# Holding the second megabyte of block 0's tokens until the second 512 KB of its first megabyte has landed, instead of the first

## The chip, the cores and the metric

The kernel runs on one core of a Trainium2 chip. The metric is the device time of one execution in microseconds (us), as the median of several runs. All data is 32-bit floating point except the two lists of ids.

## The reference, cut to what matters

x holds 64 sequences of 64 tokens with 1024 features each. Every sequence has an adapter id and a language id.

```python
# layer 0: a rank-16 adapter chosen per sequence
Bx  = einsum('bni,bri->bnr', x, B0[ids0])
x   = x + einsum('bnr,bor->bno', Bx, A0[ids0])
# layer 1: a dense product, and eight rank-16 experts with a top-2 gate
base   = einsum('btd,od->bto', x, W)
logits = einsum('btd,ed->bte', x, Wr) + 5.0 * one_hot(ids1)
gates  = softmax over the two largest logits, 0 elsewhere
h      = einsum('btd,erd->bter', x, A1)
x      = x + base + 2.0 * einsum('bter,bte,eor->bto', h, gates, B1)
```

## The kernel before, in words

The 4096 tokens lie feature-major in memory (xT, 1024 x 4096) and are worked on in 8 blocks of 512 tokens. A block's tokens are 2 MB and arrive as two tiles x of 1 MB, for the lower and the upper half of the features. `load` (line 363) brings them in with DMAs that SP issues. The first tile of block 0 alone is cut into two DMAs of 512 KB. Two blocks form a super-block; the dense product W is computed on super-blocks with a scheme that makes seven products out of eight, some of them cut again in the same way.

For each block k the steps are these, by their names in the code and in the profile:

- `gather` (397): an indirect DMA that POOL issues fetches the block's adapter rows, gb (from the B table) and ga (from the A table), 512 KB each.
- `turn` (424): TensorE transposes gb in eight pieces into PSUM (pt), in two groups of four; ScalarE copies each group into bt.
- `project` (445): pb = bt times x, in two halves over the features, so the second half needs the second tile of x. VectorE masks pb into bx.
- `adapt` (477): px = ga times bx, once for the lower and once for the upper half of the features; VectorE adds px into x in four parts per half.
- `rows` (515): ph = x times a_sb (the experts' first matrices, and behind them wr_c, the router's weights), one strip of 128 tokens after the other. Then come the gates, and the products with W (pw, pa, pb, pf).

Two DMAs are held back by small copies on POOL. `hold` in `load` writes one column of the second tile of block 0's tokens with a value read from the first tile; the DMA that fills the second tile must come after this copy, and the copy after the data it reads. `hold` in `consts` (309) does the same for a_sb with a value of gb of block 0. `spread`, also in `consts`, copies wr_c behind a_sb on POOL.

The order of the instructions on each engine isn't the order of the code. Each step is given to a planner, the class `Plan`, with a cost for each engine that could do it, what it reads and writes, the buffers that it takes, and a due time `at` (lower is more urgent). `order` (64) goes through the steps with its own estimate of time, and each engine then executes its steps in that order. The estimates rest on constants: LAG 0.2 between engines, 350 KB per us for DMA with LAND 1.8 behind it, GATHER 1.5 for an indirect DMA before LAND, and start times SET for SP, DVE and POOL. Of the steps that an engine could start within LOOK (0.2) of the earliest one, it takes the one with the lowest due time (lines 140 and 141):

```python
t0 = min(can[e])[0][0]
_, n, t = min((steps[n]["at"], n, t) for (t, _), n in can[e] if t <= t0 + self.LOOK)
```

`behind` says that a step isn't planned before another one has begun. Block 0's ga is behind the second tile of x, block 1's gb behind a_sb, and so are block 1's tokens and W. The due times at the start: gb of block 0 -61, its x and ga -60, the hold of a_sb -56, a_sb and the spread -45, gb of block 1 -43, pt of block 0 -40, pb -38, px -37 and -36, ph -14 to -11, pt of block 1 -12. Of PSUM buffers there are four l (pt, pb, ph, and px of four parts at a time), two a and two b (px of block 0's upper half takes these four). There is one bt.

Of the kernel before, what the change touches and what calls it, by code (L numbers as in the profile page):

```python
# [174 lines left out]
def kernel(  # L175
# [58 lines left out]
    HC = NC // 2  # L234
# [19 lines left out]
    act, pool, sp = Pinned(tc, nc.scalar), Pinned(tc, nc.gpsimd), Pinned(tc, nc.sync)  # L254
# [14 lines left out]
    def new(tag, shape, name):  # L269
        return pools[tag].tile(shape, F32, tag=tag, name=name)  # L270
# [81 lines left out]
    made = {}  # L352

    def part(t, cs=range(HC), gs=range(NG)):
        return [(t, c, g) for c in cs for g in gs]
# [7 lines left out]
    def load(k, i, at):  # L363
        t = ("x", k, i)

        held = (k, i) == (0, 1)

        def hold(e):

            made[t] = new("q", [P, HC, TB], f"x_{k}_{i}")  # L370
            pool.tensor_copy(made[t][:, 0, :1], made["x", 0, 0][:, 0, :1])


        cuts = ((0, HC // 2), (HC // 2, HC)) if (k, i) == (0, 0) else ((0, HC),)

        def fn(c0, c1):
            if not held and c0 == 0:
                made[t] = new("q", [P, HC, TB], f"x_{k}_{i}")
            sp.dma_start(
                made[t][:, c0:c1],  # L380
                xT[(i * HC + c0) * P : (i * HC + c1) * P, k * TB : (k + 1) * TB].rearrange(
                    "(c p) t -> p c t", p=P
                ),
            )

        if held:
            plan.add(
                {"POOL": 0.2}, hold, part(("x", 0, 0), [0]), part(t), at, [("q", t)]
            )
        for c0, c1 in cuts:  # L390
            plan.add(
                {"SP": 0.5}, lambda e, c0=c0, c1=c1: fn(c0, c1),
                [], part(t, range(c0, c1)), at, [("q", t)] * (not held and c0 == 0),
                kb=256 * (c1 - c0), behind=[("a1",)] * (k == 1) + [(t, 0, 0)] * (c0 > 0),
            )
# [359 lines left out]
    def fine_weights(s, n, k, a, at):  # L755
# [33 lines left out]
        if s == FINE:  # L789
            for x in range(4):  # L790
                plan.add(
                    {"DVE": 0.29, "POOL": 0.48}, sums(x), [(a,)] + [(t, y) for y in range(x)], [(t, x)], at - 3,
                    [("s", t)] * (x == 0), sb=True,
                )
            plan.add({"SP": 0.1}, keep, [(t, x) for x in range(4)], [("fine", n, k)], at + 4, kb=256)
        else:
            plan.add({"SP": 0.1}, load, [("fine", n, k)], [(t, x) for x in range(4)], at - 6, [("s", t)], kb=256)
# [462 lines left out]
    for k, at in ((0, -60), (1, -42)):  # L1260
        load(k, 0, at)
        gather(k, "gb", b0, at - 1)
        load(k, 1, at)
        gather(k, "ga", a0, at)
        if k == 0:
            consts()
# [81 lines left out]
```

## Time and profile before

| | |
|---|---|
| median of 3 runs | 515.6 us (515.21 to 516.27) |
| profiled execution, its own time | 514.86 us |
| its span, first to last instruction | 513.0 us |
| TensorE (PE) busy | 499.8 us, 97% |
| VectorE (DVE) busy | 410.3 us, 80% |
| DMA | 110.00 MB, 214 GB/s on the mean |
| granted TensorE clock, mean | 0.999 |
| first matmul | 8.80 us after the span's start |

The times in the profile's views count from the start of the span of this one execution. It was 0.74 us quicker than the median of the runs. In a view of instructions in order of time, a line has the start, the duration, the engine, the operation and its tiles, and in brackets how long the engine sat idle before it and what released it. SPq is SP's queue of DMA issues; its durations are those of issuing, not of the transfer.

### The profile page before, as it was taken

The page shows a single profiled execution, that of the slowest core. Times are in us where ns is not written, and L with a number is a line of the kernel's source. Part 1 is how long each engine was busy: PE and PEld are TensorE (multiplying, and loading weights), DVE is VectorE, ACT ScalarE, POOL GpSimd, SP SyncE. Part 2 cuts the span into 40 slices and gives each one's busy share as a digit, 9 for nine tenths or more (in the row PEclk, how much of TensorE's full clock was granted, in tenths as well). Part 3 has the DMA queues.
Part 4 walks back from the last instruction along what each step waited for, and adds up shares of the span by engine and source line. Part 5 has one row for each costly group of instructions (what it writes and reads, how often), then busy time and mean ns, then how long its engine had stood idle before and what let it go on. Part 6 is the DMA issues. An engine that isn't in the chain of part 4 may idle for free.

```text
span 513.0 us, 9559 instructions
## 1 busy us (share of the span) xinstructions
PE 499.8 (97%) x3678; PEld 442.5 (86%) x3678; DVE 410.3 (80%) x822; ACT 75.8 (15%) x204; POOL 105.4 (21%) x175
## 2 busy tenths in 40 slices
PE   3999999999999999999999999999999999999997
PEld 2857888889888998889888998889989999999996
DVE  0788899989878777888989789874889988875964
ACT  1111100001000211111201221102301112112210
POOL 3002000020432433442233021201212120212100
PEclk9999999999999999999999999999999999999999
DMA  8999273964895648875567645972756665673023
GB/s 286 374 369 351 83 270 120 332 247 141 300 312 201 208 130 284 309 247 187 185 226 236 221 131 173 356 260 81 240 173 205 231 202 142 228 192 96 0 115 132
DMA packets 60172, 110.00 MB, mean 214 GB/s; under 512 B 5600, under 2 KB 11744, under 8 KB 60128
## 3 DMA queue, kind: packets, MB, share of 16 engines
q1 hardware_dynamic: 57824, 101.01, 58.7%
q0 software_dynamic: 2304, 8.39, 4.9%
q8 instruction: 29, 0.48, 0.4%
q14 instruction: 15, 0.12, 0.1%
HBM read 76.09 MB, written 33.29 MB: 213 GB/s over the span
## 4 chain that ended last, share of the span: by engine, by line
PE 94%; DMA 4%; DVE 1%; issue 0%; SPq 0%
PE pa L29 38%; PE pb L29 19%; PE pf L29 16%; PE ph L29 12%; PE px L29 3%; PE pw L29 3%; DMA x<-in_xT 3%; PE pt L29 2%; DMA gb<-in_b,idx 1%; PE pg L29 1%; DVE s L29 0%; DMA ids_sb<-in_ids 0%; DVE ti L29 0%; DVE u L29 0%; DVE x L29 0%
## 5 line engine op out<-in xcount | busy, mean ns | idle before, releaser
L29 PE MATMUL pa<-ti,s 128*128 128x256 f32 x432 | 102.1, 380 | 0.0
L29 PEld LDWEIGHTS pa<-ti,s 128*128 128x128 f32 x432 | 78.7, 190 | 9.3
L29 ACT COPY cp<-pf 128x128 f32<-128x128 f32 (+1 forms) x123 | 37.0, 302 | 214.4 <-PE pf L29 201.3
L29 PEld LDWEIGHTS ph<-a_sb,x 128*128 128x128 f32 x512 | 61.7, 190 | 1.5 <-issue 0.9
L29 PE MATMUL ph<-a_sb,x 128*128 128x136 f32 x512 | 62.5, 279 | 0.2 <-issue 0.2
L29 PE MATMUL pb<-ti,s 128*128 128x256 f32 x224 | 55.8, 380 | 0.0
L29 PE MATMUL pa<-x,s 128*128 128x256 f32 x216 | 52.7, 381 | 0.0
L29 PE MATMUL pf<-tt,sf 128*128 128x128 f32 x246 | 47.5, 277 | 0.0
L29 DVE TENSOR_TENSOR x<-px,x 128x512 f32<-128x512 f32 x64 | 39.9, 683 | 6.8 <-PE px L29 6.8
L29 PEld LDWEIGHTS pb<-ti,s 128*128 128x128 f32 x224 | 40.9, 190 | 4.8 <-issue 0.2
L29 PEld LDWEIGHTS pf<-tt,sf 128*128 128x128 f32 x246 | 41.4, 191 | 3.8 <-issue 0.4
L29 PEld LDWEIGHTS pa<-x,s 128*128 128x128 f32 x216 | 39.3, 190 | 5.0 <-issue 0.4
L29 PE MATMUL pa<-t,s 128*128 128x256 f32 x168 | 41.2, 380 | 0.0
L29 PEld LDWEIGHTS pa<-t,s 128*128 128x128 f32 x168 | 30.8, 190 | 3.9 <-issue 0.2
L29 POOL TENSOR_TENSOR tt<-ti 128x256 f32<-128x256 f32 x16 | 12.3, 771 | 93.5 <-PE pf L29 60.2
L29 DVE TENSOR_TENSOR o<-pa,u 128x512 f32<-128x512 f32 x32 | 22.0, 687 | 9.9 <-PE pa L29 9.6
L29 POOL TENSOR_TENSOR tt<-x 128x256 f32<-128x256 f32 x11 | 9.2, 833 | 93.9 <-PE pf L29 47.7
L29 DVE TENSOR_TENSOR o<-pb,o 128x512 f32<-128x512 f32 x35 | 23.1, 687 | 2.7 <-PE pb L29 1.9
L29 DVE TENSOR_TENSOR ti<-t 128x512 f32<-128x512 f32 x24 | 16.7, 696 | 8.4 <-PE pb L29 6.4
L29 DVE TENSOR_TENSOR ti<-x,ti 128x512 f32<-128x512 f32 x30 | 21.7, 724 | 1.2 <-PE pb L29 0.6
L29 DVE TENSOR_TENSOR o<-o,cp 128x256 f32<-128x256 f32 x46 | 19.6, 425 | 2.5
L29 POOL TENSOR_TENSOR sf<-s 128x128 f32<-128x128 f32 x27 | 14.0, 518 | 35.8 <-DMA s<-s_kept 14.5
(154 smaller groups left out, 807.6 us busy)
## 6 DMA issues: line engine op xcount, KB each, us to landing
s<-s_kept SPq DMA_DIRECT2D x147, 256.0 KB
x<-in_xT SPq DMA_DIRECT2D x15, 1024.0 KB
out_T<-o SPq DMA_DIRECT2D x30, 512.0 KB
s_kept<-s SPq DMA_DIRECT2D x28, 256.0 KB
sf<-f_kept SPq DMA_DIRECT2D x27, 256.0 KB
s_kept<-w SPq DMA_DIRECT2D x18, 256.0 KB
w<-in_w SPq DMA_DIRECT2D x16, 256.0 KB
f_kept<-sf SPq DMA_DIRECT2D x14, 256.0 KB
```

The lines of the kernel that those rows point to most:

```text
L29: return self._tc.keep_in_program_order(f(*args, **kwargs))
```

## The change

The hold of the second tile reads its value from another place of the first tile: from the first of the chunks that the second 512 KB bring (chunk HC // 2 = 2 of four), where it was chunk 0, of the first 512 KB. What the planner is told that the hold reads is changed with it. Nothing else is touched.

```diff
         def hold(e):

             made[t] = new("q", [P, HC, TB], f"x_{k}_{i}")
-            pool.tensor_copy(made[t][:, 0, :1], made["x", 0, 0][:, 0, :1])
+            pool.tensor_copy(made[t][:, 0, :1], made["x", 0, 0][:, HC // 2, :1])
...
         if held:
             plan.add(
-                {"POOL": 0.2}, hold, part(("x", 0, 0), [0]), part(t), at, [("q", t)]
+                {"POOL": 0.2}, hold, part(("x", 0, 0), [HC // 2]), part(t), at, [("q", t)]
             )
```

## The prediction

> **What bounds the kernel now.** I read the page first, then TensorE's busy time by stretches, then the chain of waits of the first 18 us, and last the order of PE, POOL and SP in those 18 us.
>
> The page's busy row, then the stretches (columns: stretch, length, busy time, instructions, granted clock, DMA share, GB/s):
>
> ```profile
> PE 499.8 (97%) x3678; PEld 442.5 (86%) x3678; DVE 410.3 (80%) x822; ACT 75.8 (15%) x204; POOL 105.4 (21%) x175
> ...
> 8.80:17.90 9.10, 8.52 (x144) 1.00 1.05 371
> 17.90:60.00 42.10, 42.06 (x333) 1.00 0.82 291
> 60.00:110.00 50.00, 49.70 (x314) 1.00 0.71 256
> 110.00:510.10 400.10, 399.56 (x2891) 1.00 0.61 198
> ```
>
> TensorE is the bound from 17.9 us on: over the 492.2 us to 510.1 it is idle 0.88 us. A moment at which its work is put off early in the kernel is hardly won back later. So the change is priced at one place: when does the first ph matmul start, now at 17.93 us? The chain says what stands before it:
>
> ```profile
> 3.08 5.59 DMA gb<-in_b,idx
> 8.66 0.14 issue
> 8.80 1.94 PE pt L29 x8
> 10.74 3.39 PE pb L29 x64
> ...
> 14.15 0.30 DVE bx L29
> ...
> 14.50 2.07 PE px L29 x64
> 16.56 1.18 PE pt L29 x8
> 17.74 0.19 issue
> 17.93 0.35 PE ph L29
> ```
>
> The first gather (gb of block 0) lands at 8.66 and starts TensorE. The px products of block 0 follow at 14.50, then pt, the eight transposes of block 1's gathered rows. Those fill a gap: ph waits for VectorE's additions of px into x, so 1.25 us of pt costs nothing where it stands. Now POOL and SP:
>
> ```profile
> 3.08 1.11 POOL L29 DMA_INDIRECT gb<-in_b,idx  x1 [1.31 <-DVE order L29]
> 5.06 0.18 POOL L29 COPY x<-x 128x1 f32<-128x1 f32 x1 [0.87 <-DMA x<-in_xT]
> 5.27 0.38 SPq L29 DMA_DIRECT2D x<-in_xT  x1
> 5.40 0.97 POOL L29 DMA_INDIRECT ga<-in_a,idx  x1 [0.16 <-issue]
> 6.59 0.24 POOL L29 COPY a_sb<-wr_c 128x64 f32<-128x64 f32 x1 [0.22 <-issue]
> 8.71 0.18 POOL L29 COPY a_sb<-gb 128x1 f32<-128x1 f32 x1 [1.88 <-DMA gb<-in_b,idx]
> 8.93 0.66 SPq L29 DMA_DIRECT2D a_sb<-in_a  x1
> 9.04 0.97 POOL L29 DMA_INDIRECT gb<-in_b,idx  x1
> ```
>
> The copy at 5.06 is the hold that is changed. Block 1's gather (9.04) has its own row, from issue to landing 6.6 us, so it lands at 15.64, just 0.85 us before TensorE takes up pt at 16.49:
>
> ```profile
> DMA to landing us min/median/max: 6.6/6.6/6.6
> ```
>
> **The change, part by part.** No instruction is added or taken away. The hold waits for the second 512 KB of block 0's first megabyte.
>
> *On the chip.* DMA moves 395 GB/s in the microsecond from 4.0, at which 512 KB take 1.33 us, and the two halves share one queue, the second behind the first. I put the hold at 6.3 instead of 5.06 (both ends: 6.0 and 6.5). Behind it on POOL stand the gather ga of block 0, the spread, the hold of a_sb, and block 1's gather; on SP the second megabyte, then a_sb, the first w and block 1's tokens. The second megabyte is issued at about 6.5, 1.2 us late.
>
> *In the order.* The planner works with its own guesses and fixes each engine's order by them; I use these only for the order, not for a time. Before: the first cut is thought to land at 4.96, hold at 5.16, second megabyte issued 5.56 and landed 10.93, hold of a_sb 7.50, block 1's gather issued 8.00 and landed 12.40. The second half of pb is put at 11.13 to 12.07, bx at 12.27 to 12.57, px at 12.77. pt of block 1 could start at 12.60 (landing plus LAG), 0.17 ahead of px: inside LOOK (0.2), so the lower due time wins and px goes first.
>
> After: the second cut is thought to land at 4.63 + 1.80 = 6.43; hold 6.63 to 6.83. The spread is ready and POOL takes it at 6.83 to 7.13, the second megabyte is issued at 7.03 and, at (7.53 + 2.93) + 1.80, landed at 12.25. ga takes POOL from 7.13 to 8.23, ahead of the hold of a_sb (its due time is lower), which comes at 8.23; a_sb is issued at 8.63, block 1's gather at 8.73, thought to land at 13.13. Second half of pb: 12.45 to 13.39. bx: 13.59 to 13.89. px: 14.09. But pt of block 1 is ready at 13.33, and can start at 13.59 (its bt buffer comes free with the end of pb, plus LAG). Now it is 0.50 ahead of px, outside LOOK, so pt goes first. It takes one of the four l slots; px of the first half needs all four, so the second pt follows too (14.03), then px of the second half, which uses the a and b slots, then px of the first half. TensorE's order becomes pb, pt, pt, px, px, ph. **This swap, not the 1.2 us, is what I price.**
>
> *The sum.* pt now stands in front of px and waits for block 1's gather. When does that land? From its issue: the first gather's landing barely moves, and POOL is at its hold by then, so issue is about 8.7 to 9.0, and 6.6 us later is 15.3 to 15.6. From the stream: DMA runs at about 370 GB/s from 7 to 18 us, the second megabyte leaves up to 1.2 us late, ga ahead of it on the same queue 1.4 us late: 15.64 + 1.2 = 16.8. I take the middle, 16.0. Then 0.14 to start (as at 8.66 to 8.80), 1.25 for eight transposes, and 14.50 to 17.93 = 3.43 from px to ph (two of VectorE's additions of one half and one of the other, as now): 16.0 + 0.14 + 1.25 + 3.43 = 20.82. Against 17.93 that is **+2.9 us**; +2.2 with 15.3, +3.7 with 16.8. With the shortest gather row (5.6 us) it would still be +1.2.
>
> What lies beside it costs nothing: the wait of pb's second half for the second megabyte (perhaps 0 to 0.7 us around 12.2) ends before the wait for the gather does, and an earlier start of TensorE is eaten by it as well. a_sb is needed only by ph and gets 2.9 us more; block 1's tokens and w likewise. If that cover were gone, a_sb's 512 KB at 1.4 us would be the price. From ph on TensorE's work is the same, so the sum stands to the end. The profiled execution took 514.86 us; with +2.9 it is 517.8. It lies 0.74 under the median of 515.6, so against runs like those I say **518.5**.
>
> *A rule against the trace.* Both groups are 64 matmuls of one shape, block 0's before 17.8 and block 1's after it (mean ns of one last, then idle before):
>
> ```profile
> L29 PE MATMUL pb<-x,bt 128*32 128x128 f32 x64 | 3.4, 402 | 0.0
> ...
> L29 PE MATMUL pb<-x,bt 128*32 128x128 f32 x64 | 2.0, 274 | 0.0
> ```
>
> The granted clock reads 1.00 in both places, yet the first runs at 53 ns each and the second at 31, and pt of block 0 took 1.94 where that of block 1 took 1.25. The Trainium skill, "TensorE: Matmul & The Clock Gate", section "Part 1: The HAM clock gate", says that the array starts at half rate and falls back to it after an idle window of some 3.4 us. TensorE would now idle from about 14.1 to 16.1. By the rule as stated 2.0 us are too short, so the fast durations above hold (+2.9). If it did fall back, pt costs 0.7 more and px 64 times 21 ns, 1.3: +4.9. I take the fast one.
>
> **The rivals.**
>
> *Not slower: the gather gains and the order stays.* Between 7.0 and 8.7 the second megabyte shares the engines with the tail of the first gather:
>
> ```profile
> q1 hardware_dynamic: 113, 0.23, 64.0%
> q0 software_dynamic: 51, 0.15, 36.6%
> ```
>
> This is the microsecond from 7.0; q0 is the gather. The skill's "DMA: Bandwidth & Descriptors", "Queues, rings and completion order", says that each engine goes round-robin between its queues. Alone, the 0.15 MB need 0.4 us at the 373 GB/s of that microsecond; the gather could land some 0.9 us sooner than 8.66 by the rule. The trace is less kind: its tail is short of bytes (0.01 MB after 8.0) and seems to hang on a slow ring, so I would give it 0.3. Then TensorE starts at 8.5 and pb's first half ends near 12.1. It decides whether px stays ahead of pt and whether the second megabyte has landed by 12.1: then -0.3, 515.3. Against it: the planned gap of 0.50 is well over LOOK.
>
> *Same order, and the second megabyte is the bound.* Now pb's two halves run without a gap. Issued 1.2 us later, the megabyte may land at 12.3 to 13.0, and pb waits 0.2 to 0.9 us: 516.1.
>
> *The swap, and TensorE falls back to the slow pace:* +4 to +5, 520.2. For it: the idle windows need not begin where the wait does, and the wait may be 2.7 us.
>
> *The edit does nothing*, if the hold waited for both halves already. It did not: by 5.0 us DMA had moved 0.20, 0.30 and 0.40 MB in the three microseconds from 2.0, and both halves are 1.05 MB.
>
> **How the numbers follow.** Swap at the fast pace 0.64, swap at the slow pace 0.18; order kept with the megabyte as bound 0.10; order kept with a gain 0.06; something else, such as the later order falling better, 0.02. The range, 516.4 to 520.6, holds the swap from +1.2 to +5.0 and the upper end of the third case; it leaves out the gain and the quiet part of the third, below 2 in 10. 0.2% is 1.03 us, about what a measurement of this kernel can tell from no change. Slower by more: both swaps and a little of the third, 0.84. Within: the rest of the third and most of the gain, 0.13. Faster: 0.03.
>
> **What would show it.** Right: POOL's copy at 6.0 to 6.5; the spread ahead of ga; in TensorE's order pt of block 1 directly behind pb, waiting for "DMA gb", and px after it; ph near 20.8; an end that is later by the same amount. pt at 1.25 says fast, near 1.9 slow. Wrong: px at once behind bx; a ph before 18.9; a TensorE that makes up time after 21 us; or block 1's gather landed before 14.5.

## The result and the profile after

The changed kernel takes 520.52 us (median of 10 runs, 517.95 to 522.05), against 515.64 for the kernel before (10 runs, 515.01 to 517.61). The ratio is 1.0084 with a 95% interval of 1.0063 to 1.0105: 4.3 us slower, 3.2 to 5.4 (the two medians lie 4.9 apart, inside that interval). The profiled execution has a span of 518.4 us, where that of before has 513.0.

TensorE's busy time by stretches, of the kernel after:

```profile
8.65:23.30 14.65, 8.91 (x140) 1.00 1.04 362
23.30:60.00 36.70, 36.66 (x308) 1.00 0.83 289
60.00:110.00 50.00, 50.00 (x291) 1.00 0.62 220
110.00:515.10 405.10, 405.03 (x2942) 1.00 0.60 200
```

From the first ph (now 23.34 us) to 515.1 TensorE is idle for 0.1 us. All of the loss lies ahead of it: ph was at 17.93, so it comes 5.41 us later, and the span is 5.4 us longer. The chain that ended last, cut to the first 24 us:

```profile
1.66 4.55 DMA x<-in_xT
6.21 0.06 issue
6.27 0.18 POOL x L29
...
6.47 10.45 DMA x<-in_xT
16.93 0.14 issue
17.06 1.94 PE pb L29 x32
19.00 1.05 PE pt L29 x4
20.04 2.12 PE px L29 x64
22.16 1.18 issue
23.34 0.70 PE ph L29 x4
```

Before, this chain began with the gather of gb. Now it runs through the tokens: the second half of the first megabyte to 6.21, the hold at 6.27, and then the second megabyte, under way for 10.45 us. TensorE had begun in time, and then stood (start, duration, and in brackets the idle time before and what released it):

```profile
8.65 1.94 PE L29 MATMUL pt<-ident,gb 128*128 128x128 f32 x8 [8.65 <-DMA gb<-in_b,idx]
10.52 1.94 PE L29 MATMUL pb<-x,bt 128*32 128x128 f32 x32
17.06 1.94 PE L29 MATMUL pb<-x,bt 128*32 128x128 f32 x32 [4.61 <-DMA x<-in_xT]
18.93 1.12 PE L29 MATMUL pt<-ident,gb 128*128 128x128 f32 x4
19.97 2.19 PE L29 MATMUL px<-bx,ga 32*128 32x128 f32 x64
23.34 0.93 PE L29 MATMUL ph<-a_sb,x 128*128 128x136 f32 x6 [1.18 <-issue]
```

The swap is there: pt of block 1 stands between pb and px. Only its first four transposes do; the other four come after the first two strips of ph. But pt doesn't wait here. Block 1's gather has landed at 16.71 by the trace's signals, a little ahead of 16.93, when pb at last gets its second megabyte. Two waits end almost together, and the experiments have to take them apart.

The order on POOL, after:

```profile
6.27 0.18 POOL L29 COPY x<-x 128x1 f32<-128x1 f32 x1 [2.17 <-DMA x<-in_xT]
6.46 0.24 POOL L29 COPY a_sb<-wr_c 128x64 f32<-128x64 f32 x1
6.85 0.97 POOL L29 DMA_INDIRECT ga<-in_a,idx  x1
8.57 0.18 POOL L29 COPY a_sb<-gb 128x1 f32<-128x1 f32 x1 [0.75 <-DMA gb<-in_b,idx]
8.90 0.97 POOL L29 DMA_INDIRECT gb<-in_b,idx  x1 [0.15 <-issue]
```

The megabyte's landing is counted by sixteen signals, one for each part. In the trace of before they come between 10.24 and 11.77 us. After, fifteen come between 11.12 and 12.85, and the last at 16.93. Block 0's ga runs beside the megabyte both times, but it meets it at another point. Before, half of the megabyte's packets had started by 8.8 us, and ga's packets (4 KB each) came from 9.6 to about 12. After, half had started by 9.9, ga's packets came from 10.7 to about 14, and those of block 1's gather right behind them.

### The profile page after: what moved, and what is told of

Read it like the earlier page. It is cut to its first block, busy times and chain, and to the rows that moved or that the text cites. A ratio compares the mean times of both kernels' runs of the same rounds, so it can differ in the third digit from the quotient of the medians.

```text
span 518.4 us, 9557 instructions
## 1 busy us (share of the span) xinstructions
PE 500.6 (97%) x3678; PEld 442.9 (85%) x3678; DVE 409.5 (79%) x822; ACT 76.0 (15%) x204; POOL 105.2 (20%) x175
## 4 chain that ended last, share of the span: by engine, by line
PE 95%; DMA 4%; issue 0%; SPq 0%; DVE 0%; POOL 0%
PE pa L29 39%; PE pb L29 20%; PE pf L29 16%; PE ph L29 11%; DMA x<-in_xT 4%; PE px L29 3%; PE pw L29 3%; PE pt L29 1%; PE pg L29 1%; SPq L29 0%; DVE o L29 0%; POOL x L29 0%; POOL a_sb L29 0%
## 5 line engine op out<-in xcount | busy, mean ns | idle before, releaser
L29 PE MATMUL pb<-x,bt 128*32 128x128 f32 x512 | 18.4, 293 | 4.7 <-DMA x<-in_xT 4.6
```

The lines of the kernel that those rows point to most:

```text
L29: return self._tc.keep_in_program_order(f(*args, **kwargs))
```

## The experiments

Theory A is the prediction's: the swap costs. Theory B: the late megabyte itself costs. Theories C and D came up after the first four runs, for why the megabyte lands so late: C, gathers that run beside it hold up its last part; D, that part is slow by itself.

**Order only.** The planner is told of the second half, the copy reads the first. All five engines then have exactly the changed kernel's order.

```diff
-                {"POOL": 0.2}, hold, part(("x", 0, 0), [0]), part(t), at, [("q", t)]
+                {"POOL": 0.2}, hold, part(("x", 0, 0), [HC // 2]), part(t), at, [("q", t)]
```

> The planner is told of the second half, the copy on POOL reads the first: every engine has the changed kernel's order, but the second megabyte is issued at about 5.3 us as before. Theory A (the order: pt of block 1 in front of px waits for block 1's gather): pb ends near 14.1 as before, pt starts at 15.7 to 16.8 when the gather lands, px behind it, ph near 20; 517.4 to 518.6 us. Theory B (the second megabyte itself comes late and holds up pb's second half): nothing is left of the loss, 515.6 to 516.0, and px starts before 15 us.

519.26 us (6 runs, 518.28 to 520.75), ratio 1.0069 (1.0054 to 1.0083). TensorE:

```profile
10.38 1.94 PE L29 MATMUL pt<-ident,gb 128*128 128x128 f32 x8 [10.38 <-DMA gb<-in_b,idx]
12.25 3.94 PE L29 MATMUL pb<-x,bt 128*32 128x128 f32 x64
17.48 0.66 PE L29 MATMUL pt<-ident,gb 128*128 128x128 f32 x4 [1.28 <-DMA gb<-in_b,idx]
18.06 2.07 PE L29 MATMUL px<-bx,ga 32*128 32x128 f32 x64
21.30 3.94 PE L29 MATMUL ph<-a_sb,x 128*128 128x136 f32 x32 [1.17 <-issue]
```

pb has no gap, and pt waits for block 1's gather: theory A's wait, without theory B's. The time is a little above A's upper end, and the wait of pt isn't all of the loss. TensorE also began late: the first gather landed at 10.25, and so POOL issued block 1's gather at 10.64, where it had been 9.04:

```profile
10.64 0.97 POOL L29 DMA_INDIRECT gb<-in_b,idx  x1 [0.15 <-issue]
```

pb ended at 16.19. With px next, ph would have come near 20.0 by an estimate (0.40 for bx, 3.43 from px to ph, as before). So of the 3.4 us by which ph is later than 17.93 the swap is worth some 1.3 in this profile, and the late first gather most of the rest. Why that gather landed late is not shown: in two profiles of the kernel before, whose megabyte is issued as early, it landed at 8.66 and 9.30.

**Wait only.** The copy reads the second half, the planner is told of the first. All engines have the order of before.

```diff
-            pool.tensor_copy(made[t][:, 0, :1], made["x", 0, 0][:, 0, :1])
+            pool.tensor_copy(made[t][:, 0, :1], made["x", 0, 0][:, HC // 2, :1])
```

> The copy on POOL waits for the second half, the planner is told of the first: every engine has the order of before, with px ahead of pt, but the second megabyte is issued at about 6.5 us. Theory A: pb waits at most a microsecond, ph before 19 us, 515.6 to 516.6 us. Theory B: one part of the second megabyte lands near 17 us as in the changed kernel's profile, pb's second half starts there, ph near 22 to 23, 519 to 521 us.

520.62 us (11 runs), ratio 1.0067 (1.0036 to 1.0099). The runs fall in two groups: three at 514.6 to 516.8, eight at 520.3 to 522.0. The profile is of the upper one:

```profile
8.70 1.94 PE L29 MATMUL pt<-ident,gb 128*128 128x128 f32 x8 [8.70 <-DMA gb<-in_b,idx]
10.57 1.69 PE L29 MATMUL pb<-x,bt 128*32 128x128 f32 x32
16.24 1.93 PE L29 MATMUL pb<-x,bt 128*32 128x128 f32 x32 [3.99 <-DMA x<-in_xT]
18.58 3.72 PE L29 MATMUL px<-bx,ga 32*128 32x128 f32 x64 [0.41 <-DVE bx L29]
22.23 1.09 PE L29 MATMUL pt<-ident,gb 128*128 128x128 f32 x8
23.67 1.51 PE L29 MATMUL ph<-a_sb,x 128*128 128x136 f32 x11 [0.35 <-issue]
```

So theory B holds as well: the wait alone loses most of what both halves lose. Twelve parts of the megabyte were in by 11.61, the other four landed between 14.76 and 16.11. A second thing shows. px takes 3.72 us, 2.07 before. The stretches of this kernel (the last three columns are granted clock, DMA share, GB/s):

```profile
8.70:12.20 3.50, 3.50 (x40) 1.00 0.95 337
12.30:15.30 3.00, 0.00 (x0) 1.00 1.04 362
16.20:18.20 2.00, 1.93 (x32) 0.50 1.09 374
18.50:22.10 3.60, 3.52 (x64) 0.50 1.04 384
22.30:24.00 1.70, 1.35 (x12) 1.00 1.04 349
```

While TensorE waits, it is put back to half rate, and pb's second half and px run at that pace.

**The changed kernel, px first.** One more dependence in the plan restores px ahead of pt.

```diff
-            {"PE": 0.44}, fn, [(("gb", k),)] + [(bt, 0)] * g, [(pt,)] ...
+            {"PE": 0.44}, fn, [(("gb", k),)] + [(bt, 0)] * g + [(("px", 0, 1, 0),)] * (k == 1), [(pt,)] ...
```

> The changed kernel with one more dependence in the plan: pt of block 1 is planned behind px of block 0, so TensorE's order is that of before, while POOL keeps the changed order (spread ahead of ga). Theory A: as the wait alone, 515.6 to 516.6 us. Theory B: 519 to 521 us, and pb's second half waits 3 to 5 us for the second megabyte.

520.61 us (8 runs: three at 515.6 to 516.1, five at 520.0 to 521.4), ratio 1.0053 (1.0019 to 1.0087). The profile is of the upper group:

```profile
17.19 1.94 PE L29 MATMUL pb<-x,bt 128*32 128x128 f32 x32 [4.58 <-DMA x<-in_xT]
```

Theory B again. Without the swap there are also runs at the time of the kernel before, which neither the ten runs of the changed kernel nor the five that follow show (the lowest is 517.95).

**The changed kernel again.**

> The changed kernel once more, to see whether the 4.6 us wait of pb for the second megabyte comes back in another profile. Theory A: the wait varies and the time follows the gather of block 1, ph at 20 to 21 where the megabyte is on time. Theory B: the wait for the megabyte is again 3 to 5 us and ph is near 23; median 519.5 to 521 us.

520.34 us (5 runs, 519.62 to 521.82). This profile has both waits in turn, and a slow px:

```profile
14.50 1.94 PE L29 MATMUL pb<-x,bt 128*32 128x128 f32 x32 [1.77 <-DMA x<-in_xT]
17.39 1.12 PE L29 MATMUL pt<-ident,gb 128*128 128x128 f32 x4 [0.96 <-DMA gb<-in_b,idx]
18.44 3.23 PE L29 MATMUL px<-bx,ga 32*128 32x128 f32 x64
22.59 2.67 PE L29 MATMUL ph<-a_sb,x 128*128 128x136 f32 x21 [0.92 <-issue]
```

The megabyte landed at 14.36, sooner than 16.93, and still ph is at 22.59: behind it stands the gather, landed at 17.35. A miss for both texts: B had the long wait back, A a ph at 21.

**Late hold, ga first.** The wait of the change, px put ahead of pt as in the run with px first, and ga issued right behind the first gather. The cut shows the last of these three edits. The later part of the plan shifts too.

```diff
-            behind=[(("x", 0, 1), 0, 0)] * ((tag, k) == ("ga", 0)) + [("a1",)] * (k == 1) + ...
+            behind=[("a1",)] * (k == 1) + ...
```

> The second megabyte waits for the second half as in the changed kernel; TensorE keeps px ahead of pt; but block 0's second gather (ga) is issued right behind the first, ahead of the hold, so it no longer runs beside the second megabyte. Theory C (the late megabyte's last part is held up by gathers that share its queue's engines): the megabyte is in before 13 us, pb's second half waits under 1 us, ph before 19 us, 515.3 to 516.8 us. Theory D (that part is slow by itself, whatever runs beside it): the wait of 4 to 5 us stays, 519 to 521 us.

516.41 us (22 runs, 515.03 to 521.43), ratio 1.0020 (1.0002 to 1.0038). In the profile, of a run in the upper part (517.59), ga was issued at 4.46 and the megabyte landed at 14.51 (the last line is a stretch, with the granted clock after the count):

```profile
14.64 1.11 PE L29 MATMUL pb<-x,bt 128*32 128x128 f32 x32 [1.98 <-DMA x<-in_xT]
16.14 3.39 PE L29 MATMUL px<-bx,ga 32*128 32x128 f32 x64 [0.39 <-DVE bx L29]
...
15.70:18.90 3.20, 2.81 (x55) 0.50 1.07 379
```

Most of the loss is gone, not all. The median is where theory C had it; this profile is not, as C had the megabyte in before 13 and ph before 19 (it is at 20.91).

**No gather beside.** The wait only, and a second copy keeps ga and all that follows on POOL until the megabyte is in.

```diff
+            if (tag, k) == ("ga", 0):
+                pool.tensor_copy(made[tag, k][:, :1], made["x", 0, 1][:, 0, :1])
             pool.indirect_dma_start(
```

> Before's order, the second megabyte waits for the second half, and a second small copy makes ga (and everything that POOL issues behind it) wait until the second megabyte has landed: no gather runs beside it. Theory C: pb's second half starts before 13.3 us; then px waits for ga, which is issued near 12 and lands 7 to 8 us later, ph near 23, 519.5 to 522 us. Theory D: pb's second half starts only at 15 to 17 us and ga lands at 23 or later, ph after 26, above 523 us.

520.78 us (4 runs, 520.39 to 521.61), where theory C had it; the reading is in pb:

```profile
10.61 1.94 PE L29 MATMUL pb<-x,bt 128*32 128x128 f32 x32
13.17 1.08 PE L29 MATMUL pb<-x,bt 128*32 128x128 f32 x32 [0.63 <-DMA x<-in_xT]
18.07 3.80 PE L29 MATMUL px<-bx,ga 32*128 32x128 f32 x64 [3.81 <-DMA ga<-in_a,idx]
```

The hold was as late as in the changed kernel (6.38), and all sixteen parts are in between 10.93 and 13.04. So theory D is out. But this run took more away than ga and block 1's gather: the hold of a_sb stands behind ga on POOL, so a_sb was issued at 15.24 (8.78 in the changed kernel), and SP's later transfers behind it. Whether the gathers or these held up the last parts has to come from elsewhere.

**Early hold, ga first.** As the run with the late hold and ga first, but with the hold of before.

> The hold of before (first half), ga issued right behind the first gather, px ahead of pt. Theory C: nothing runs beside the second megabyte but the tail of the first gather; px does not wait for ga; 515.0 to 516.0 us, as before or a little faster. Theory D: the same as before too, 515.5 to 516.5.

516.99 us (20 runs, 514.74 to 519.97), ratio 1.0024 (1.0009 to 1.0039): slower, outside what either theory said. In the profile the first gather lands at 10.02 and TensorE starts at 10.16. It is no better version.

**The kernel before again.**

> The kernel before, once more with a profile: the second megabyte in before 12.4 us, so that pb's two halves run without a gap, px at 14 to 15 us, ph near 18.

515.75 us. A small miss: pb waits 0.61 for the megabyte (landed 13.35) and ph is at 18.40. This kernel too is near the edge here: of the 41 runs of it that were taken then, one took 521.22 us (and a stray one, 2992.85, is left out of every ratio).

**Swap, ga first.** The changed kernel with ga right behind the first gather.

> The changed kernel, swap and all, with block 0's ga issued right behind the first gather, so that it is not beside the second megabyte. If swap and megabyte each cost on their own and only overlap, the megabyte is in by 13 to 14.5 us, pb is done by 16, and the first pt still waits for block 1's gather (landed 16 to 17.5); ph at 20.5 to 22, 517.8 to 520 us, and no runs near 515.5. If only the megabyte mattered, 515.5 to 517 us as with px first.

521.31 us (6 runs, 518.14 to 524.31), higher than I had it. In the profile (518.89):

```profile
13.45 1.42 PE L29 MATMUL pb<-x,bt 128*32 128x128 f32 x32 [0.17 <-DMA x<-in_xT]
16.51 0.66 PE L29 MATMUL pt<-ident,gb 128*128 128x128 f32 x4 [1.65 <-DMA gb<-in_b,idx]
17.10 2.07 PE L29 MATMUL px<-bx,ga 32*128 32x128 f32 x64
20.34 3.94 PE L29 MATMUL ph<-a_sb,x 128*128 128x136 f32 x32 [1.17 <-issue]
```

With the megabyte in time (13.31) the swap's own wait stands alone at 1.65 us, and no run is near 515.5. It also bears on theory C: a_sb and w were issued while the megabyte was under way, at 9.60 and 10.30, and only ga was gone from beside the megabyte. This kernel's later order differs too, and its profile has a further wait of 1.2 us at a later pa that the others lack; so its time is not the swap's alone, and what made the slower runs slow stays open.

**Block 1's gather held.** As the wait only, but that gather is issued when the megabyte is in; ga stays where it was.

```diff
+            if (tag, k) == ("gb", 1):
+                pool.tensor_copy(made[tag, k][:, :1], made["x", 0, 1][:, 0, :1])
             pool.indirect_dma_start(
```

> Before's order with the second megabyte held for the second half, ga where it was, but block 1's gather is issued only when the second megabyte has landed. If ga alone is enough to hold up the last part, the megabyte is in at 14 to 16 us; if it takes ga and block 1's gather one behind the other, it is in by 14. Block 1's gather then lands 7 us later, at 20.5 to 22, and pt, which stands between px and ph, waits for it: ph near 22.5 to 24, 519 to 521.5 us.

525.95 us (4 runs), 4 us above the text: the gather landed at 24.26, not by 22. The megabyte was in at 15.31, its first twelve parts by 11.88. So the last parts are held up without block 1's gather too. ga and SP's later transfers were beside them here; where ga was moved away and those transfers stayed (the two runs with late hold and ga first), the megabyte was in at 13.31 and 14.51.

**The wait only, twice more.**

> The late hold with before's order, one more look. Its times fell in two groups, 514.6 to 516.8 and 520.3 to 522.0 us. If the groups are the megabyte's last part, a look in the low group has pb's second half start before 14 us and ph before 19, one in the high group at 15 us or later and ph after 22.5.

> The same once more: low group with pb's second half before 14 us, high group with it at 15 us or later.

521.89 and 521.25 us, both of the upper group; pb's second half starts at 17.13 and 17.61 after 4.70 and 5.00 of idle, ph at 23.75 and 24.76. No profile of the lower group was obtained, so that its megabyte is in time is likely, not shown.

## Why the prediction was right, and where its steps failed

*The bound, and that a late ph stays to the end.* Right. Span less the start of ph is 495.1 us before and after, and 494.5 to 496.6 in all fourteen profiles.

*The edit on the chip.* Right: hold at 6.27 where 6.3 was put, megabyte issued at 6.47, the spread ahead of ga.

*The swap.* Right in what decides: pt of block 1 is planned in front of px, waits for block 1's gather where the megabyte is in time (in the changed kernel's first profile nothing of that wait is left), and the order alone costs 3.1 us (519.26 less 516.13, the median of before that was taken with it), against +2.9. That the two are so near is in part luck: in its profile some 1.3 us are the swap's, by the estimate above, and most of the rest is a late first gather, which the changed kernel itself doesn't have (8.51). Wrong in a detail: I let the second pt follow at 14.03. But px of the upper half could start at 14.09, inside LOOK, and has the lower due time; so only four transposes precede px. The gather came at 16.71 and 17.35, where I took 16.0; its row from issue to landing is 7.8 us now, 6.6 before:

```profile
DMA to landing us min/median/max: 7.8/7.8/7.8
```

*"What lies beside it costs nothing: the wait of pb's second half ... ends before the wait for the gather does."* This step failed. I gave that wait 0 to 0.7 us around 12.2. It was 4.61 in the first profile and 1.77 in the second, and by itself, without the swap, it costs about as much as the order alone (ratio 1.0067 against 1.0069). I had scaled the megabyte's time as one stream. Its landing is the landing of the last of sixteen parts, and moved 1.2 us later, more of it was still to come when ga's packets began (at 10.7), and block 1's followed from about 14. The rule that I had cited for the rival, that each engine goes round-robin between its queues (the Trainium skill, "DMA: Bandwidth & Descriptors", "Queues, rings and completion order"), was the one to apply to the megabyte as well; I used it for the gather alone. In the trace, between 12.4 and 16.1 us, the megabyte's last packets start 0.235 us apart, with one exception, and take 0.084 each. The difference of 0.151 fits one 4 KB packet of a gather (0.159 us), and behind each of the fifteen that are followed at this distance a 4 KB packet starts, 0.08 us later. The trace doesn't name the engine of a packet, so that they alternate on one engine is read from this spacing, not shown directly. That the long wait goes when everything is kept away from the megabyte is shown by the run with no gather beside; that it is ga more than SP's later transfers, by the spacing and the profiles with ga first.

*The slow pace.* I called 2.0 us of idle too short for the half rate and took the fast durations. The times of the trace's clock events explain it: full rate is first recorded from 13.7 us before, and from 20.3 and 20.9 in the two profiles of the changed kernel. The column reads 1.00 ahead of the first event, whatever the pace. So TensorE had not fallen back; it had not come up to speed before the wait began. In the nine profiles in which full rate came before any long wait, it came 2.9 to 5.6 us after the first matmul (4.9 before); in the five in which a wait of 1.77 to 4.70 us came first, 11.6 to 13.0 us after it. The half of pb that took 1.08 at full rate (no gather beside) took 1.94 in the changed kernel's first profile, and four transposes took 1.12 for 0.60: some 1.4 us more than at full rate. My sign (pt at 1.25 fast, near 1.9 slow) reads slow. In the second profile px took 3.23 for 2.07. Where full rate had been reached, it did fall back: after waits of 3.8 to 5.0 us for 6.8 us (0.50 in the rows above), and with the late hold and ga first after a wait of only 1.98 us, for 3.4 us, which cost px 1.3 us (3.39 for 2.07). So an idle time shorter than the 3.4 us that I cited is no safe ground for the fast durations: the measurement goes against the rule as I read it.

*The sum.* +2.9 was short of the measured +4.3 (3.2 to 5.4). The median, 520.52, lies 0.08 us inside the range, whose upper end of 520.6 was there for a TensorE that falls back, not for a late megabyte. The direction, the place (all ahead of the first ph) and the swap were foreseen; that the number held was in part luck. In the first profile: pb's second half starts at 17.06, and takes 1.94; pt 1.05; px to ph 3.30 (20.04 to 23.34); that is 23.34. My 20.82 had the gather's landing in place of the first two terms.

*The rivals.* The "not slower" one had something to it. With ga not moved ahead, the first gather landed at 8.49 to 8.79 in eight profiles with the late hold, and at 8.66, 9.30 and 10.25 with the early one; with ga ahead at 9.09 and 9.34 (late) and 10.02 (early). But a TensorE that starts sooner then waits for the megabyte. "Same order, and the second megabyte is the bound" was the right place and far too cheap: it gave the wait 0.2 to 0.9 us, and the three profiles of the wait only have 3.99 to 5.00. The slow pace, put at 520.2, came nearest to the measured 520.52. The pace was there, but as one not yet left, and the megabyte's wait wasn't in that sum.

## What to carry to other kernels

A transfer's landing is that of its last part, so when its start is moved, ask which other queue will now run beside it, and cost the last part, not the mean rate. When two waits are created by one edit, undo each by itself: here the order alone and the wait alone each cost over 3 us, and both together 4.3, since the two waits run at the same time. And an edit of what a planner is told is an edit of the order, even when the order isn't touched by hand.

## What the runs showed of the hardware

- One part in sixteen of a 1 MB transfer landed 4.1 us after the fifteenth (16.93 against 12.85), with a gather beside it; with the gathers and all later transfers kept away, all parts landed within 2.1 us. In the wait-only profile it was four parts, 3.2 us behind the twelfth (14.76 against 11.61). That the two groups of times, some 5 us apart, come from this is likely, not shown.
- A gather of 512 KB took 4.1 us from issue to landing where all DMA together moved 55 GB/s at its start and 265 later (13.87 to 17.93, no gather beside), and 7.8 in the changed kernel, where it was 259 to 387 from 8 us on.
- The granted clock column can read 1.00 while TensorE runs at half pace: ahead of the trace's first clock event it says nothing (13.7 us before, 20.3 after). The same 64 px matmuls took from 2.07 to 3.80 us. Durations of equal groups are the better witness there.
